# Two-layer image block on one core: the border between images rebuilt, and TensorE in written order

## The chip, the cores and the metric

The kernel runs on one core of a Trainium2 chip. A core has a matrix engine (TensorE, "PE" in the profile, with "PEld" for its weight loads), a vector engine (VectorE, DVE), an activation engine (ScalarE, ACT), a general engine (GpSimd, POOL) and an engine that here only issues transfers (SyncE, SP). Each engine takes its instructions in a fixed order, and waits for the others by semaphores. GpSimd, ScalarE and SyncE can each issue DMA transfers, on queues of their own. The metric is device time in microseconds, the median of several runs.

## What is computed

32 images of 96 channels x 56 x 56 pass through two layers. Both normalise each group of three channels, then add a branch to the image. Cut to what matters:

```python
# layer 0
v = gn(x)                                  # 32 groups of 3 channels
h = act_q(bn(conv1x1(v, quant(w1))))       # 96 -> 576 channels, 4 bits
h = act_q(bn(depthwise3x3(h, quant(w2))))  # 576 channels, 4 bits
x = x + v + bn(conv1x1(h, quant(w3)))      # 576 -> 96 channels
# layer 1, on v = gn(x), in three parts of 32 channels
x_0, x_05, x_1 = v[:32], v[32:64], v[64:]
x_0  = conv3x3(x_0, conv0_w * gate(mean(x_0)))                  # spatial
gap  = mean(x_05); alpha = 0.1 + 0.8 * sigmoid(mlp(gap))
Fre  = frft2d(x_05, F(alpha), F(alpha))                         # fractional Fourier
Mix  = conv1x1(Fre, conv05_w * gate(gap))
x_05 = abs(frft2d(Mix, F(-alpha), F(-alpha)))
x_1  = irfft2(conv1x1(rfft2(x_1), conv1_w * gate(mean(x_1))))   # Fourier
x = x + v + conv3x3(concat(x_0, x_05, x_1), conv2_w)            # 96 -> 96
```

## The kernel before

The outer loop takes the images one after the other. `layer0(i)` and `layer1(i)` don't issue anything; they return lists of steps (a cost and a function). `interleave` merges two lists by their costs, and so the convolution of image i is written out mixed with layer 1 of image i-1. The order of writing isn't the order on the engines: the framework's scheduler puts each engine's instructions in an order of its own, and pools of buffers add waits.

Layer 0 of an image, in the names of the profile:

- `norm`: bn_stats on VectorE, then `group_stats` (L284 on): two small matmuls (pma, pva) average over a group, and GpSimd takes the power -0.5 (L305). `split` and `base` make vh and vl, two parts of the normalised image in four phases (even and odd rows and columns).
- `expand(b, k)`: tile pe, 4 matmuls (L371), 20 of them (5 blocks b of 128 channels, 4 phases k). ACT quantises to qte (L312), DVE clips to q1s (L314), and four transfers (two in the last block) copy q1s into the padded tile qp, 32 channels each (L384; 72 copies per image, all issued by SP). There are two tiles qp.
- `depthwise(b, j)`: tile pd, 8 matmuls (L397), 18 of them, one for each 32 channels; it needs all four phases of its block in qp. ACT makes qtd, DVE makes q2.
- `project(h, lo, hi)`: tile pp (L413), two halves in four pieces each, then four DVE updates of x (L425), and `stats` (bn_stats, L429).

Layer 1 of an image: `norm` (pmb, pvb, then xs on DVE and ACT, L468 and L472; a copy flipped in both directions, called Jx here, on DVE, L479 and L487; the padded spatial part xq on ACT and DVE, L494 and L496), `gates` (ph, pg, pa, po, L500 to L519, with hid and the sigmoids on ACT, then products on DVE), `angles` (table by the sine on ACT, pj and pvv, L571 to L587, and vv sent into two rows of xs), `mix_t` (px, L608), `mix_f` (pm, L641, its result z goes to DRAM and comes back as zh and az), `spatial` (ps, L707), `hilbert` (pr), `rows_f` (pi, L667), `columns_f` (pz, L683), `final` (pc, L727, 7 chunks of 8 rows, each added to x by DVE at L735), and `store`.

Tiles pe, pd and pp share a pool of two PSUM buffers ("pair"); all small tiles, px to pc, share four ("bank"). ACT has to read a pe or pd before the next but one can start.

What is called the border here is the stretch from the last pp of one image to the last matmul of pvv of layer 1. Before, the border is written as `interleave(nxt["first"], one[-3:] + end)`: the first four expansions of the next image, the last three pc chunks of the previous one, and its store. The norm of layer 1 stands at the head of the next round, and the scheduler puts pc_4 to pc_6 ahead of pmb. The image is loaded and stored in three transfers each, issued by POOL, since the channel groups of 32 are kept in swapped order (`groups`, `perm`).

Of the kernel before, what the change touches and what calls it, by code (L numbers as in the profile page):

```python
# [59 lines left out]
HN = PN // 2  # L61
L = 57
# [38 lines left out]
def block_kernel(ctx: ExitStack, tc: tile.TileContext, out: bass.AP, a: dict):  # L101
# [21 lines left out]
    groups = ((0, 2 * G), (G, G), (2 * G, 0))  # L123
    xts = {}

    def load(i):
        xt = xp.tile([C, HW], F32, tag="x", name=f"x{i}")
        for p, c in groups:
            nc.gpsimd.dma_start(out=xt[p : p + G, :], in_=x_in[i, c : c + G].rearrange("c h w -> c (h w)"))
        xts[i] = xt  # L130
# [11 lines left out]
    def prepare():  # L142
# [90 lines left out]
        cw1 = signed("cw1", "coef1")  # L233
        cw2 = signed("cw2", "coef2")
        return w1, dw, w3, A1, B1, A2, B2, A3, B3, cw1, cw2

    w1, dw, w3, A1, B1, A2, B2, A3, B3, cw1, cw2 = prepare()
# [19 lines left out]
    for k in range(2):  # L257
        t = cp.tile([128, 4, PT], FP8, tag=f"qp{k}", name=f"qp{k}")
        nc.gpsimd.memset(t, 0.0)
        qps.append(t)  # L260
# [13 lines left out]
    g1s, css = [], []  # L274
# [3 lines left out]
    for k in range(2):  # L278
        t = cp.tile([128, 128], F32, tag=f"g1{k}", name=f"g1{k}")
        nc.scalar.dma_start(out=t[bias], in_=a["bias1"])  # L280
        nc.vector.tensor_tensor(t[bias], t[bias], bcoef[bias], ALU.mult)
        g1s.append(t)
        t = cp.tile([128, 3 * W], F32, tag=f"cs{k}", name=f"cs{k}")
        nc.vector.memset(t, 0.0)  # L284
        css.append(t)
# [38 lines left out]
    def layer0(i):  # L324
# [42 lines left out]
        def expand(b, k):  # L367
            ps = pair(f"pe{i}_{b}_{k}")
            for n, v in enumerate((s["vh"], s["vl"])):
                for h in range(2):  # L370
                    nc.tensor.matmul(  # L371
                        ps[:, h, :HN],
                        w1[:, 128 * b : 128 * (b + 1)],
                        v[:, k, HN * h : HN * (h + 1)],
                        start=(n == 0),
                        stop=(n == 1),
                    )
            src = q1s[turn["q1s"] % 3]
            turn["q1s"] += 1
            quant_act(ps, A1[:, b : b + 1], B1[:, b : b + 1], src[:, :, :PH], f"e{i}_{b}_{k}")  # L380

            n, at = blk(b) // G, PW * (k // 2) + k % 2
            for g in range(n):
                nc.sync.dma_start(  # L384
                    out=qps[(NB * i + b) % 2][G * k : G * (k + 1), g, at : at + PH * PW],
                    in_=src[g * G : (g + 1) * G].rearrange("c h w -> c (h w)"),
                )

        def depthwise(b, j):
            g = 4 * b + j  # L390
            if g == 0:
                s["q2"] = p1.tile([128, NG0, PN], BF16, tag="q2", name=f"q2_{i}")
            ps = pair(f"pd{i}_{g}")
            for t in range(4):
                for h in range(2):
                    at = PW * (t // 2 + PH // 2 * h) + t % 2
                    nc.tensor.matmul(  # L397
                        ps[:, h, :HN],
                        dw[:, g, t, :],
                        view(qps[(NB * i + b) % 2][:, j, :], at, [[PW, PH // 2], [1, PH]]),  # L400
                        start=(t == 0),
                        stop=(t == 3),
                    )
            quant_act(ps, A2[:, g : g + 1], B2[:, g : g + 1], s["q2"][:, g, :], f"d{i}_{g}")
# [26 lines left out]
        def first(b):  # L431
            return [(0.75, lambda k=k: expand(b, k)) for k in range(4)]

        conv = []
        for b in range(NB):
            part = []
            nxt = first(b + 1) if b + 1 < NB else []
            for k in range(max(len(nxt), blk(b) // G)):  # L440
                part += nxt[k : k + 1]
                if k < blk(b) // G:
                    part.append((1.45, lambda b=b, k=k: depthwise(b, k)))
            conv.append(part)
# [3 lines left out]
        last.append((0.0, stats))  # L448
# [3 lines left out]
            "first": first(0),  # L452
            "conv": conv,
            "last": last,
# [3 lines left out]
    def layer1(i):  # L458
# [3 lines left out]
        def norm():  # L462
# [4 lines left out]
            ff, fr = slice(0, G), slice(G, 2 * G)  # L467
# [6 lines left out]
            for at, src, dims in (  # L474
                (W + 1, n * W + n, [W, 1]),
                (1, n, [1]),
                (W, n * W, [W]),
            ):
                nc.vector.tensor_scalar(  # L479
                    view(xs[fr], at, [[d, n] for d in dims]),  # L480
                    view(xt[ff], src, [[-d, n] for d in dims]),
                    mean[ff],
                    rstd[ff],
                    ALU.subtract,
                    ALU.mult,
                )
            nc.vector.tensor_scalar(xs[fr, 0:1], xt[ff, 0:1], mean[ff], rstd[ff], ALU.subtract, ALU.mult)  # L487
            sp = slice(2 * G, C)
# [9 lines left out]
        def gates():  # L498
# [31 lines left out]
            for k in range(4):  # L530
                nc.vector.tensor_tensor(
                    view(tmp[fr], 128 * k, [[4, 32], [1, 4]]),
                    view(cw1[fr], 128 * k, [[4, 32], [1, 4]]),
                    view(sg[fr], 0, [[1, 32], [32, 4]]),
                    ALU.mult,
                )
            g1 = g1s[i % 2]
            nc.vector.tensor_reduce(g1[fr], view(tmp[fr], 0, [[4, 128], [1, 4]]), AX.X, ALU.add)

            for k in range(2):  # L540
                nc.vector.tensor_tensor(
                    view(tmp[: 2 * G], 128 * k, [[4, 32], [1, 4]]),
                    view(cw2, 128 * k, [[4, 32], [1, 4]]),
                    view(sg[: 2 * G], 128, [[1, 32], [32, 4]]),
                    ALU.mult,
                )
# [9 lines left out]
        def angles():  # L556
# [17 lines left out]
            cs = css[i % 2]  # L574
            s["cs"] = cs
# [39 lines left out]
        def hilbert(g):  # L615
# [10 lines left out]
            for r in range(4):  # L626
                src = ps[G * r : G * (r + 1), : 2 * W * n].rearrange("p (q u w) -> p q u w", u=2, w=W)
                at = (1 + 32 * g + 2 * r) * (W + 2) + 1
                dst = view(cat[:G].rearrange("p h w -> p (h w)"), at, [[8 * (W + 2), n], [W + 2, 2], [1, W]])
                if r % 2:  # L630
                    nc.vector.tensor_copy(dst, src)
                else:
                    nc.scalar.copy(dst, src)

        def mix_f(j):
# [5 lines left out]
            nc.tensor.matmul(ps[:, :CN], g1s[i % 2][2 * G : 3 * G + 2], s["xs"][2 * G : 3 * G + 2, at], start=True, stop=True)  # L641
# [19 lines left out]
        def rows_f(g):  # L661
# [4 lines left out]
            for k in range(4):  # L666
                nc.tensor.matmul(  # L667
                    ps[:W, 2 * W * k : 2 * W * (k + 1)], zh[:, 4 * g + k, :], s["cs"][: 64 + W, W : 3 * W], start=True, stop=True
# [5 lines left out]
        def columns_f(g):  # L674
# [5 lines left out]
            for k in range(n):  # L680
                q = 4 * (4 * g + k)
                for t in range(2):
# [3 lines left out]
                        s["cs"][:W, W * (1 - t) : W * (3 - t)],  # L686
# [16 lines left out]
        def spatial(h):  # L703
# [10 lines left out]
            for k in range(4):  # L714
                src = ps[G * k : G * (k + 1), :HN].rearrange("p (h w) -> p h w", w=PH)
                at = (1 + PH * h + k // 2) * (W + 2) + 1 + k % 2
                dst = view(cat[2 * G : C].rearrange("p h w -> p (h w)"), at, [[2 * (W + 2), PH // 2], [2, PH]])
# [19 lines left out]
        def store():  # L737
            for p, c in groups:
                nc.gpsimd.dma_start(out=out[i, c : c + G].rearrange("c h w -> c (h w)"), in_=xt[p : p + G, :])
# [12 lines left out]
    now = layer0(0)  # L752
    interleave(now["norm"] + now["split"] + now["first"], [])
    for i in range(B + 1):
        one, end = layer1(i - 1) if i else ([], [])
        if i == B:
            interleave(one + end, [])
            break
        if i + 1 < B:
            load(i + 1)  # L760
        conv, last, nxt = now["conv"], now["last"], None
        if i + 1 < B:
            nxt = layer0(i + 1)
            conv[1] += nxt["norm"]
            conv[4][1:1] = nxt["split"]
        interleave([s for part in conv for s in part] + last, one[:-3])
        interleave(nxt["first"] if nxt else [], one[-3:] + end)
        now = nxt
# [35 lines left out]
def _constants():  # L804
# [4 lines left out]
    perm = np.r_[64:96, 32:64, 0:32]  # L809
    k = {}  # L810
    group = perm // 3
# [29 lines left out]
    k["coef1"] = coef1.reshape(128, 512).astype(f)  # L841
# [8 lines left out]
    k["coef2"] = coef2.reshape(64, 256).astype(f)  # L850
    return perm, k


def _layout(inputs):
# [4 lines left out]
    perm, k = _constants()  # L859
# [11 lines left out]
    k["w1"][:, :HID] = g0("w1")[:, perm, 0, 0].T  # L871
# [12 lines left out]
    k["w3"] = np.tile(g0("w3")[perm, :, 0, 0].T.reshape(NG0, G, C).swapaxes(0, 1), (4, 1, 1)).reshape(128, NG0 * C)  # L884
# [3 lines left out]
    k["vec96"] = np.stack([g0(n)[perm] for n in ("b3", "g3", "be3", "m3", "v3")], axis=1)  # L888
# [5 lines left out]
    k["cw1"] = np.tile(by_parts(g1("conv05_w"))[None, :, None], (4, 1, 4, 1, 1)).reshape(128, 512)  # L894
# [4 lines left out]
    k["cw2"] = np.tile(by_parts(g1("conv1_w"))[None, :, None], (2, 1, 2, 1, 1)).reshape(64, 256)  # L899
# [3 lines left out]
    start = {"alpha": G, "gfreq": G, "gsp": 2 * G, "gfft": 0}  # L903
# [23 lines left out]
    k["wc"] = g1("conv2_w")[perm][:, perm].transpose(1, 2, 3, 0).reshape(C, 9 * C)  # L927
    k["bc"] = g1("conv2_b")[perm][:, None]
# [19 lines left out]
```

## Time and profile before

| what | value |
|---|---|
| median of 3 runs | 5584.15 us (5581.7 to 5593.18) |
| profiled execution | 5580.95 us |
| its span | 5579.2 us |
| mean granted clock of TensorE | 0.842 |
| one image, pmb to pmb (2023.2 to 2194.2 us) | 171.0 us |
| x loads: 96 of 392 KB, issue to landing | 6.0 us |
| out stores: 96 of 392 KB, issue to landing | 5.3 us |

A line of a group reads: line, engine, operation, output<-inputs, shape, count; then busy time and the mean of one in ns; then the engine's idle time just before these instructions and what ended most of it. "Clock" is the share of full speed that TensorE was granted: at 0.5 the same matmul takes twice as long, and counts as busy for all of it. An image is 1.2 MB, in three transfers of 392 KB each way.

### The profile page before, as it was taken

How to read it: one execution, taken by the hardware profiler on the slowest of the kernel's cores; microseconds unless marked ns; L12 is line 12 of the kernel's file. 1: busy time of each engine (PE TensorE's matmuls, PEld its weight loads, DVE VectorE, ACT ScalarE, POOL GpSimd, SP SyncE). 2: the span in 40 equal slices, each digit the busy share in tenths (PEclk: the TensorE clock that was granted, in tenths of full speed). 3: DMA queues.
4: the chain of work that ended last, by engine and by line, in shares of the span. 5: the costliest groups of instructions: out<-in, count | busy, mean ns of one | idle time of the engine just before them, and what ended most of it. 6: DMA issues, size and time to landing. Idle time of an engine off the chain costs nothing.

```text
span 5579.2 us, 65275 instructions
## 1 busy us (share of the span) xinstructions
PE 4954.7 (89%) x24384; PEld 3090.9 (55%) x24384; DVE 2410.1 (43%) x5355; ACT 2161.8 (39%) x2824; POOL 176.0 (3%) x270
## 2 busy tenths in 40 slices
PE   4988899889998898998889988889888899889897
PEld 2555555555555555555555555556555555555554
DVE  6444434444444444344444444444444434344432
ACT  3433434433334334344333443343443334433421
POOL 2000000000000000000000000000000000000000
PEclk9788888888988888888889888888888898888887
DMA  2121212221212212122212122121221121221111
GB/s 61 38 54 39 43 42 43 54 53 30 53 33 54 54 39 43 42 44 54 53 30 53 33 53 54 38 44 35 51 54 47 36 51 34 54 54 32 41 33 39
DMA packets 394080, 249.79 MB, mean 45 GB/s; under 512 B 284053, under 2 KB 386917, under 8 KB 387621
## 3 DMA queue, kind: packets, MB, share of 16 engines
q1 hardware_dynamic: 381696, 165.68, 13.8%
q0 software_dynamic: 9216, 77.08, 5.9%
q8 instruction: 194, 3.18, 0.2%
q10 hardware_dynamic: 2852, 2.85, 0.2%
q14 instruction: 122, 0.99, 0.1%
HBM read 92.77 MB, written 89.92 MB: 33 GB/s over the span
## 4 chain that ended last, share of the span: by engine, by line
PE 80%; ACT 9%; DMA 5%; DVE 4%; SPq 1%; issue 1%; ACTq 0%; POOL 0%; DVEq 0%; POOLq 0%
PE pc L727 27%; PE pd L397 16%; PE px L608 6%; PE pe L371 6%; PE ps L707 5%; PE pz L683 5%; PE pi L667 4%; PE pp L413 4%; ACT qtd L312 4%; DMA qp<-q1s 4%; PE pm L641 3%; SPq L384 1%; ACT xq L494 1%; ACT xs L472 1%; PE pr L625 1%
## 5 line engine op out<-in xcount | busy, mean ns | idle before, releaser
L727 PE MATMUL pc<-cat,wc 96*96 96x448 f32 x4032 | 1565.9, 540 | 1.0 <-ACT cat L701 1.0
L397 PE MATMUL pd<-qp,dw 128*128 128x392 fp8e4 x4608 | 1063.0, 378 | 393.3 <-DMA qp<-q1s 221.7
L727 PEld LDWEIGHTS pc<-cat,wc 96*96 96x96 f32 x4032 | 650.8, 163 | 766.4 <-issue 759.1
L312 ACT ACTIVATE qte<-pe,o,s 128x784 int16<-128x784 f32 x640 | 635.6, 998 | 1050.2 <-PE pe L371 618.6
L312 ACT ACTIVATE qtd<-pd,o,s 128x784 int16<-128x784 f32 x576 | 577.3, 1002 | 1024.3 <-PE pd L397 992.1
L397 PEld LDWEIGHTS <-dw 128*128 128x128 fp8e4 x4608 | 464.8, 105 | 892.1 <-issue 555.5
L371 PE MATMUL pe<-vh,w1r 96*128 96x392 f32 x1280 | 497.4, 474 | 26.1 <-ACT vh L360 21.7
L314 DVE TENSOR_SCALAR q<-qtd 128x784 bf16<-128x784 int16 x576 | 209.5, 364 | 711.1 <-ACT qtd L312 710.3
L735 DVE SCALAR_TENSOR_TENSOR x<-pc,bc,x 96x448 f32<-96x448 f32 x224 | 152.0, 679 | 784.6 <-PE pc L727 784.6
L314 DVE TENSOR_SCALAR q1s<-qte 128x784 fp8e4<-128x784 int16 x640 | 364.4, 570 | 276.9 <-ACT qte L312 255.0
L371 PE MATMUL pe<-vl,w1r 96*128 96x392 f32 x1280 | 366.2, 370 | 0.0
L608 PE MATMUL px<-g,xs 64*112 64x64 f32 x1792 | 351.4, 393 | 0.0
L608 PEld LDWEIGHTS px<-g,xs 64*112 64x112 f32 x1792 | 339.2, 302 | 19.3 <-issue 19.3
L371 PEld LDWEIGHTS pe<-vh,w1r 96*128 96x128 f32 x1280 | 273.0, 218 | 130.2 <-issue 71.3
L707 PE MATMUL ps<-xq,g 128*128 128x392 f32 x512 | 299.1, 749 | 0.0
L683 PE MATMUL pz<-cs,Y 56*128 56x112 f32 x1792 | 264.4, 318 | 13.7 <-ACT Y L671 13.7
L371 PEld LDWEIGHTS pe<-vl,w1r 96*128 96x128 f32 x1280 | 267.9, 214 | 0.4 <-DVE vl L361 0.4
L683 PEld LDWEIGHTS pz<-cs,Y 56*128 56x128 f32 x1792 | 255.9, 230 | 20.8 <-ACT Y L671 20.8
L641 PE MATMUL pm<-xs,g 34*128 34x448 f32 x448 | 222.9, 642 | 17.5 <-ACT zs L646 17.3
L667 PE MATMUL pi<-cs,zh 120*56 120x112 f32 x2048 | 211.9, 262 | 7.7 <-DMA zh<-z 7.7
L413 PE MATMUL pp<-q,w3q 32*96 32x392 bf16 x4608 | 212.3, 330 | 3.8 <-ACT qtd L312 2.8
L707 PEld LDWEIGHTS ps<-xq,g 128*128 128x128 f32 x512 | 145.2, 298 | 122.7 <-issue 112.0
(149 smaller groups left out, 4214.0 us busy)
## 6 DMA issues: line engine op xcount, KB each, us to landing
qp<-q1s SPq DMA_DIRECT2D x2304, 26.2 KB
z<-zs SPq DMA_DIRECT2D x224, 224.0 KB
x<-in_x_dram POOLq DMA_DIRECT2D x96, 392.0 KB, 6.0
out_dram<-x POOLq DMA_DIRECT2D x96, 392.0 KB, 5.3
zh<-z SPq DMA_DIRECT2D x64, 392.0 KB
az<-z SPq DMA_DIRECT2D x256, 98.0 KB
xs<-vv SPq DMA_DIRECT2D x64, 12.2 KB
prep<-in_w_dram ACTq DMA_DIRECT2D x1, 864.0 KB
```

The source lines that it names most:

```text
L312: nc.scalar.activation(t.rearrange("p (h n) -> p h n", h=2), ps[:, :, :HN], AF.Relu, bias=offset, scale=scale)
L314: nc.vector.tensor_scalar(dst, src, 15.0, None, ALU.min, saturate=False if dst.dtype == FP8 else None)
L371: nc.tensor.matmul(ps[:, h, :HN], w1[:, 128 * b : 128 * (b + 1)], v[:, k, HN * h : HN * (h + 1)], start=(n == 0), stop=(n == 1),)
L397: nc.tensor.matmul(ps[:, h, :HN], dw[:, g, t, :], view(qps[(NB * i + b) % 2][:, j, :], at, [[PW, PH // 2], [1, PH]]), start=(t == 0), stop ...
L413: nc.tensor.matmul(s["pp"][k // 2][:C, k % 2, :HN], w3[rows, g, :], s["q2"][rows, g, HN * h : HN * (h + 1)], start=(g == 0), stop=(g == NG ...
L608: nc.tensor.matmul(ps[: 2 * W, 64 * k : 64 * (k + 1)], s["xs"][: 2 * G, at : at + 2 * W], s["g2"], start=True, stop=True)
L641: nc.tensor.matmul(ps[:, :CN], g1s[i % 2][2 * G : 3 * G + 2], s["xs"][2 * G : 3 * G + 2, at], start=True, stop=True)
L667: nc.tensor.matmul(ps[:W, 2 * W * k : 2 * W * (k + 1)], zh[:, 4 * g + k, :], s["cs"][: 64 + W, W : 3 * W], start=True, stop=True)
L683: nc.tensor.matmul(ps[:, 2 * W * k : 2 * W * (k + 1)], s["Y"][:, t, q : q + 4, :].rearrange("p h c -> p (h c)"), s["cs"][:W, W * (1 - t) : ...
L707: nc.tensor.matmul(ps[:, :HN], s["g0"][:, 128 * k : 128 * (k + 1)], view(xq, PH // 2 * h * (W + 2) + k, [[W + 2, PH // 2], [2, PH]]), star ...
L727: nc.tensor.matmul(ps[:C, :CN], wc[:, C * t : C * (t + 1)], cat[:, CR * j + dy : CR * j + dy + CR, dx : dx + W], start=(t == 0), stop=(t = ...
L735: nc.vector.scalar_tensor_tensor(part, ps[:C, :CN], bc, part, ALU.add, ALU.add)
```

## The change

It does seven things:

1. The swapped order of channels goes (`groups`, `perm`), and with it the split in three: one load and one store per image, both issued by SP. The load of image i+2 is issued after the border, in place of image i+1's at the head of the round.
2. The flipped copy Jx is done by GpSimd.
3. Expansion runs seven steps ahead of the depthwise step (`LEAD = 7`): the first seven of 20 stand at the border, then one depthwise and one expansion in turn. There are three tiles qp.
4. The copies q1s to qp with odd number go by GpSimd's queue, those with even number by SP's (36 and 36 per image).
5. The tiles g1 and cs exist once and not twice; two coefficient tables are one.
6. The border is written with layer 1's norm first, then seven expansions with the last two pc chunks; the last pp pieces are mixed with pc_3 and pc_4. The next image's norm and split are at other places of the round.
7. `manual_schedule` for TensorE: its instructions are issued in the order written; the other engines are still ordered by the scheduler.

```diff
-        for p, c in groups:
-            nc.gpsimd.dma_start(out=xt[p : p + G, :], in_=x_in[i, c : c + G].rearrange("c h w -> c (h w)"))
+        nc.sync.dma_start(out=xt, in_=x_in[i].rearrange("c h w -> c (h w)"))
...
-    for k in range(2):
+    for k in range(3):
         t = cp.tile([128, 4, PT], FP8, tag=f"qp{k}", name=f"qp{k}")
...
-                nc.sync.dma_start(
-                    out=qps[(NB * i + b) % 2][G * k : G * (k + 1), g, at : at + PH * PW],
+                (nc.gpsimd if g % 2 else nc.sync).dma_start(
+                    out=qps[(NB * i + b) % 3][G * k : G * (k + 1), g, at : at + PH * PW],
                     in_=src[g * G : (g + 1) * G].rearrange("c h w -> c (h w)"),
...
+        ex = [(0.75, lambda b=b, k=k: expand(b, k)) for b in range(NB) for k in range(4)]
+        de = [(1.45, lambda g=g: depthwise(g // 4, g % 4)) for g in range(NG0)]
         conv = []
-        for b in range(NB):
...
+        for g in range(NG0):
+            conv += de[g : g + 1] + ex[LEAD + g : LEAD + g + 1]
...
-                nc.vector.tensor_scalar(
-                    view(xs[fr], at, [[d, n] for d in dims]),
+                nc.gpsimd.tensor_scalar(
+                    view(xs[G : 2 * G], at, [[d, n] for d in dims]),
...
     now = layer0(0)
+    if B > 1:
+        load(1)
     interleave(now["norm"] + now["split"] + now["first"], [])
...
-            conv[1] += nxt["norm"]
-            conv[4][1:1] = nxt["split"]
-        interleave([s for part in conv for s in part] + last, one[:-3])
-        interleave(nxt["first"] if nxt else [], one[-3:] + end)
-        now = nxt
+            conv[8:8] = nxt["norm"]
+            at = 2 * (4 * NB - LEAD) + 1
+            conv[at:at] = nxt["split"]
+        interleave(conv, one[:-4])
+        interleave(now["last"], one[-4:-2])
+        two, done = layer1(i)
+        interleave(two[:1] + (nxt["first"] if nxt else []), one[-2:] + end)
+        if i + 2 < B:
+            load(i + 2)
+        one, end, now = two[1:], done, nxt
+    interleave(one + end, [])
...
-    with tile.TileContext(nc) as tc:
+    with tile.TileContext(nc) as tc, tc.manual_schedule(engines={mybir.EngineType.PE}):
```

Written out, TensorE's work at the new border is: the last piece of pp, pmb, pvb, pc_5, the four pe of block 0, pc_6, three pe of block 1, pd_0, then ph, pg, pa, po, pj, pvv, then the fourth pe of block 1, px_0, pd_1, px_1 and so on.

## Prediction

> **What bounds the kernel now.** The page first: busy times, the chain that ended last, the costliest groups.
>
> ```profile
> PE   4954.7 (89%) x24384; PEld 3090.9 (55%) x24384; DVE 2410.1 (43%) x5355; ACT 2161.8 (39%) x2824; POOL 176.0 (3%) x270
> PE 80%; ACT 9%; DMA 5%; DVE 4%; SPq 1%; issue 1%; ACTq 0%; POOL 0%; DVEq 0%; POOLq 0%
> L397 PE MATMUL pd<-qp,dw 128*128 128x392 fp8e4 x4608 | 1063.0, 378 | 393.3 <-DMA qp<-q1s 221.7
> L312 ACT ACTIVATE qtd<-pd,o,s 128x784 int16<-128x784 f32 x576 | 577.3, 1002 | 1024.3 <-PE pd L397 992.1
> ```
>
> TensorE bounds it. It idles mostly before pd (393.3 us), of which the q1s copies end 221.7, or 7.2 per image. But busy is not busy at full speed, so the next view is one image cut into stages (pmb to pmb, 171.0 us; columns: stretch, length, PE, PEld, DVE, ACT, POOL busy, granted clock, DMA share, GB/s).
>
> ```profile
> 2023.20:2061.70 38.50, 25.34 (x98) 14.94 (x97) 20.69 (x52) 22.12 (x23) 3.54 (x7) 0.67 0.36 83
> 2061.70:2086.60 24.90, 24.18 (x97) 17.35 (x97) 9.34 (x20) 6.73 (x11) 0.00 (x0) 0.64 0.13 40
> 2086.60:2097.00 10.40, 10.40 (x50) 7.22 (x51) 3.81 (x8) 4.53 (x9) 0.00 (x0) 0.80 0.31 106
> 2097.00:2128.20 31.20, 28.69 (x182) 22.91 (x182) 11.82 (x34) 17.78 (x27) 0.56 (x1) 0.89 0.41 60
> 2128.20:2172.40 44.20, 44.20 (x273) 22.69 (x272) 22.52 (x44) 12.57 (x18) 0.00 (x0) 1.00 0.02 5
> 2172.40:2194.20 21.80, 21.74 (x68) 11.03 (x67) 6.02 (x12) 3.83 (x4) 0.56 (x2) 1.00 0.06 16
> ```
>
> TensorE works 154.55 of 171.0 us; 13.2 of the 16.45 idle lie in the first row, the border between images. By the matmul rows at full clock one image is: pc 7 x 6.77 = 47.4, pd 18 x 1.38 = 24.8, pe 20 x 0.713 = 14.3, pp 6.2, px 5.4, ps 5.4, pz 6.3, pi 6.4, pm 5.7, pr 3.3, small ones 2.5: 127.7. So 26.9 us are lost to half clock and 16.45 to waiting. Both prices matter.
>
> **What brings the clock back.** Cut into steps of 3.413 us on the grid of the clock's own changes, every step shows 1.0 or 0.5. It falls after a step with half or less to do. It doesn't rise after every full one. Two full steps that stayed at half (all engines), each followed by one that is still at half:
>
> ```profile
> 3657.53:3660.95 3.42, 3.42 (x11) 2.53 (x11) 2.35 (x6) 1.82 (x3) 0.00 (x0) 0.50 0.06 15
> 3660.95:3664.36 3.41, 3.41 (x6) 1.47 (x5) 0.00 (x0) 3.36 (x5) 0.00 (x0) 0.50 0.02 6
> ...
> 4268.52:4271.93 3.41, 3.27 (x11) 2.13 (x10) 3.38 (x6) 2.83 (x2) 0.00 (x0) 0.50 0.06 16
> 4271.93:4275.35 3.42, 2.34 (x10) 2.31 (x11) 2.30 (x10) 3.39 (x3) 0.00 (x0) 0.50 0.00 0
> ```
>
> The first held 1.85 us of ps (128 rows) and 1.64 of pz (56 rows): by rows 1.85 + 1.64 x 56/128 = 2.57 of 3.41. The second held 1.49 of pd and 1.77 of pe (96 rows): 2.82. Of 78 steps of px alone (64 rows) none raised it. Steps that did raise it begin at 2.85 (2.63 pd, 0.29 pe); ps alone did in 46 of 46. So the bar lies near 2.83, an estimate from these rows. No step of before starts at half clock with pc alone (96 rows): it would reach 3.41 x 0.75 = 2.56, under the bar, as would pe alone.
>
> **Part by part, per image.** The written order is: last pp, pmb, pvb, pc_5, four pe, pc_6, three pe, pd_0, gates ph to pvv, then px, pd and pe mixed, pm, ps.
>
> (a) Statistics. Before, pc_4 to pc_6 lie between the last pp and pmb. Now nothing does. Rows: four x updates 2.2, four bn_stats 2.2, bn_aggr 0.33, then pmb to pvb 1.15 and small steps: 6.1 us idle. Any grid of 3.41 us has a nearly empty step in it, so the clock is at half when pc_5 starts. Bounds 5.5 to 6.6.
>
> (b) pc_5 to pd_0 then hold 13.5 + 7 x 0.713 + 1.38 = 19.9 us of full-speed work, 96 rows but for the last 1.4. Below the bar all of it doubles: +19.9. If pc does raise the clock after one step, +3.4 (1.7 more work time, about as much lost again at the next boundary). I take 19.9, by the 2.57 row, the nearest to 2.56. One more us for pe_0_2, whose pair buffer waits for ACT.
>
> (c) Gates and angles. Before fills them in part; with TensorE in written order nothing stands between ph and pvv. The end of before shows this chain bare (columns: start, length, engine, operation, idle before):
>
> ```profile
> 5439.97 0.26 PE L500 MATMUL ph<-stb,mw 96*32 96x1 f32 x2 [1.75 <-DVE stb L306]
> 5440.57 1.22 PE L505 MATMUL pg<-mw,hid 33*1 33x320 f32 x2 [0.34 <-ACT hid L502]
> 5447.63 1.96 PE L518 MATMUL po<-row 1*128 1x64 f32 x8 [5.43 <-DVE row L510]
> 5454.44 0.76 PE L571 MATMUL pj<-de,e 57*128 57x112 f32 x2 [4.46 <-DVE de L569]
> 5456.87 0.96 PE L587 MATMUL pvv<-v 1*56 1x112 f32 x4 [1.21 <-DVE v L582]
> ```
>
> 17.9 us from ph to the end of pvv. Four of the 5.4 before po go away, since xs and xq are done under pc_5 now; 1.1 comes on, as hid waits behind qtd_0 on ACT: 15.0, of which 2.5 is work. Idle +12.5, bounds 10 (less DVE in it) and 15.4 (nothing saved).
>
> (d) px comes up cold. Between px's a pd lifts the clock if enough of its 2.8 us falls in one step (2.25, by the bar: in 1.67 of 3.41 positions). First chance pd_1, 6.7 us in, worth 3.3; then pd_2 (7.9), pd_3 (11.2). I take 6.
>
> (e) pm (34 rows) takes the clock down again until ps_0: from the second pe after it to ps_0 are about 8 us of work. I take 6.5, bounds 3 and 9.
>
> (f) Other waits of the fixed order, no filler behind them: pva 1, pi_0 for zh 1.5, pz_0 1, pc_0 1.1, pd_15 1, pp's buffers 2.4: 8, bounds 5 and 12.
>
> (g) What goes: with expansion seven steps ahead, copies are out for over 15 us before pd needs them, against 1.85 to 5.1 us each, so the 7.2 us on copies and 5.5 on qtd go; that idle isn't in the sum. Seven pe and pc_6 are the cover; without it 7.2 come back. pz with pd and pe keeps full clock, also in the sum.
>
> (h) At nothing: one load and one store from SP, the same 1.2 MB each way as three of 392 KB (landing 6.0 and 5.3 us). The load stands behind the store's landing on SP, and behind it qp copies and the vv rows; pm, the first reader of those, is over 20 us off. Half the copies go to POOL at 0.52 per issue against 0.58, behind Jx. Jx: 2.7 us on DVE; on POOL no such row. The nearest, pow against a small DVE step (0.57 to 0.15), makes it up to 10; DVE's own 2.7 is the other end. I take 6: its reader px_0 is 50 us later. If POOL holds DVE's xs back by that, ACT's xs and xq and then pe_0_0 are late, which pc_5 at half clock (13.5) covers; at full clock about 4 show.
>
> [...]
>
> Sum: 127.7 + 6.1 + 19.9 + 1 + 12.5 + 6 + 6.5 + 8 = 187.7 against 171.0. Around the 31 periods the span has 5579.2 - 31 x 171.0 = 278.2. 31 x 187.7 + 278 = 6097 of span; the profiled run took 1.75 more than its span and the median 3.2 more than it: **6102**. Ends of the terms together reach 5650 to 6600; as they are separate, 5900 to 6290 is the forecast's own range.
>
> [...]
>
> **Rivals.** (1) pc does bring the clock back, stalls as summed: 187.7 - 19.9 + 3.4 = 171.2, with 4 for Jx 175: 5590 to 5710. For: pc never fell below 1.0 where it was warm; against: the 2.57 row. (2) Faster: pc lifts the clock in its first step, and it then lasts through px and pm, as pd and pe between them do the rest: (d) 2, (e) 2, (f) 5: 171.2 - 4 - 4.5 - 3 = 159.7, 5234; it wins as long as (b), (d) and (e) together stay under 15.7 us, against 32.4 above. For: mixed steps at full clock stayed there down to 0.48 of full rows; against: image 0's mix of px, pd and pe stayed at half for 41 us. (3) The order isn't kept or hardly changes a thing: 171, within 0.2%; against: manual order is for all of TensorE.
>
> **Numbers.** Forecast 0.73, rival 1 0.10, rival 2 0.15, rival 3 0.02. No change means within 0.2% (11 us). Faster 0.16 (rival 2 and a little of 1), same 0.03, slower 0.81. The range takes in rival 1 from 5590 and stops at 6290.
>
> **What would show it.** After pvb, pc_5 at 13 us or more with clock 0.5; about 6 us idle before pmb and 12 inside ph to pvv, most of TensorE's idle on stb, row, de and v; idle on qp<-q1s near nothing; PE busy up to about 5300 us. Wrong if pc_5 takes 7 to 10 us, or if idle stays near 16 per image.

## The result, and the profile after

The changed kernel takes 6283.26 us (median of 4, 6252.87 to 6287.67) against 5585.95 in the runs beside it: a ratio of 1.1235, 95% interval 1.1197 to 1.1273. The profiled execution has a span of 6285.9 us and a mean clock of 0.806 (0.842 before). All ratios in this document are of fast runs alone, while the median of written_filled also holds two slow ones (5923 us without them).

First the page of the changed kernel, busy times and the chain that ended last, then three groups of instructions (line, engine, operation, tiles, count; busy us, mean ns; idle before and what ended it):

```profile
PE 5289.2 (84%) x24384; PEld 3099.5 (49%) x24384; DVE 2663.1 (42%) x5224; ACT 2180.1 (35%) x2824; POOL 1110.9 (18%) x1359
...
PE 73%; DVE 13%; ACT 8%; issue 4%; DMA 1%; POOL 0%; ACTq 0%; SPq 0%; POOLq 0%
...
L390 PE MATMUL pd<-qp,dw 128*128 128x392 fp8e4 x4608 | 1037.2, 378 | 9.5 <-ACT qtd L305 9.0
...
L364 PE MATMUL pe<-vh,w1r 96*128 96x392 f32 x1280 | 503.9, 481 | 345.0 <-ACT qte L305 322.9
...
L452 DVE TENSOR_SCALAR xs<-x,stb 32x3136 f32<-32x3136 f32 x32 | 387.0, 12094 | 1.1
```

Two things went up: TensorE's idle time (span less busy: 996.7 us against 624.5), and its busy time (5289.2 against 4954.7) for the same 24384 matmuls, which is mostly time at half clock: busy time weighted by the granted clock grew only from 4219 to 4346 us. VectorE is now 13% of the chain (4%). The old wait is gone, pd idles 9.5 us instead of 393.3. A new one stands before pe, 322.9 us on ACT's qte. The last line tells where to look: VectorE's xs, one instruction per image, takes 12.1 us on average, and took 1.9 in the kernel before:

```profile
L468 DVE TENSOR_SCALAR xs<-x,stb 32x3136 f32<-32x3136 f32 x32 | 60.9, 1903 | 1.1
```

The waits of TensorE in the changed kernel (us in all, times, longest):

```profile
PE pe L364 <- ACT qte L305: 322.9, 63, 16.7
PE pmb L287 <- DVE mvb L285: 157.5, 32, 4.9
PE pj L554 <- DVE de L552: 156.5, 32, 4.9
...
PE pd L390 <- DMA qp<-q1s: 0.4, 1, 0.4
```

The second and third are the statistics chain and the gates chain, standing bare once in each of 32 images. One image cut into stages, from the last pp to the next last pp (length; PE, PEld, DVE, ACT, POOL busy; clock, DMA share, GB/s):

```profile
2061.06:2067.50 6.44, 0.83 (x6) 0.74 (x5) 5.29 (x12) 0.00 (x0) 0.00 (x0) 0.72 0.00 0
2067.50:2104.13 36.63, 26.91 (x74) 14.38 (x74) 19.76 (x15) 13.14 (x10) 20.90 (x16) 0.72 0.13 35
2104.13:2116.59 12.46, 4.73 (x26) 2.93 (x25) 8.57 (x30) 4.58 (x7) 1.81 (x4) 0.67 0.60 152
2116.59:2163.03 46.44, 45.66 (x131) 26.81 (x131) 11.71 (x31) 11.54 (x16) 4.49 (x9) 0.50 0.15 48
2163.03:2201.07 38.04, 36.61 (x244) 27.17 (x242) 15.52 (x34) 24.16 (x36) 5.48 (x11) 1.00 0.35 55
2201.07:2258.53 57.46, 54.71 (x290) 26.12 (x290) 21.54 (x41) 14.55 (x20) 1.49 (x3) 0.94 0.02 4
```

The rows are: statistics; pc_5 to pd_0; gates and angles; px to ps_0; pr to ps_1; pc_0 to the last pp. The border (rows 1 to 3) holds 23.1 us of idle, and row 4 runs whole at half clock: 45.66 us busy for some 22.8 of work. From row 5 on little is lost. After the first, the images take from 191 to 198 us; this one, of 197.5, is among the longer ones.

Inside row 2, the timeline of the changed kernel (start, length, engine, operation):

```profile
2067.50 10.30 PE L708 MATMUL pc<-cat,wc 96*96 96x448 f32 x18
...
2068.66 14.62 POOL L463 TENSOR_SCALAR xs<-x,stb 32x3025 f32<-32x3025 f32 x3
2068.77 12.10 DVE L452 TENSOR_SCALAR xs<-x,stb 32x3136 f32<-32x3136 f32 x1
...
2080.88 0.16 DVE L455 SCALAR_TENSOR_TENSOR nmr<-stb 96x1 f32<-96x1 f32 x1
2080.96 2.18 DVE L480 TENSOR_SCALAR xq<-x,stb 32x1512 f32<-32x1512 f32 x2
2081.14 2.99 ACT L456 ACTIVATE xs<-x,nmr,stb 32x3136 f32<-32x3136 f32 x1 [42.95 <-DVE nmr L455]
...
2084.14 3.35 ACT L478 ACTIVATE xq<-x,nmr,stb 32x1568 f32<-32x1568 f32 x2
2087.52 1.90 ACT L305 ACTIVATE qte<-pe,o,s 128x784 int16<-128x784 f32 x2
...
2088.58 0.70 PE L364 MATMUL pe<-vh,w1r 96*128 96x392 f32 x1 [9.34 <-ACT qte L305]
```

VectorE's xs starts 0.1 us after GpSimd's Jx and ends 12.1 us later. Behind it stands nmr, for which ACT waits; then ACT does its own xs and xq (6.3 us) and only then qte. pe_0_2 waits 9.34 us for that with both its buffers full. And pc_5 itself takes 10.3 us, neither the 6.8 of full clock nor the 13.5 that was expected of it.

### The profile page after: what moved, and what is told of

Its sections match the earlier page's. It is cut to its first block, busy times and chain, and to the rows that moved or that the text cites. A ratio compares the mean times of both kernels' runs of the same rounds, so it can differ in the third digit from the quotient of the medians.

```text
span 6285.9 us, 66280 instructions
## 1 busy us (share of the span) xinstructions
PE 5289.2 (84%) x24384; PEld 3099.5 (49%) x24384; DVE 2663.1 (42%) x5224; ACT 2180.1 (35%) x2824; POOL 1110.9 (18%) x1359
## 4 chain that ended last, share of the span: by engine, by line
PE 73%; DVE 13%; ACT 8%; issue 4%; DMA 1%; POOL 0%; ACTq 0%; SPq 0%; POOLq 0%
PE pc L708 22%; PE pd L390 15%; PE pe L364 8%; PE px L589 6%; PE pm L622 6%; DVE xs L452 4%; PE pz L664 4%; PE pp L406 4%; PE pi L648 3%; DVE x L418 2%; PE ps L688 2%; ACT qtd L305 2%; ACT xq L478 2%; ACT cat L682 2%; ACT qte L305 2%
## 5 line engine op out<-in xcount | busy, mean ns | idle before, releaser
L708 PE MATMUL pc<-cat,wc 96*96 96x448 f32 x4032 | 1721.9, 585 | 32.6 <-ACT cat L682 32.6
L377 POOL DMA_DIRECT2D qp<-q1s x1152 | 586.0, 512 | 3382.9 <-DVE q1s L307 2202.3
L708 PEld LDWEIGHTS pc<-cat,wc 96*96 96x96 f32 x4032 | 706.0, 178 | 945.9 <-issue 894.6
L390 PE MATMUL pd<-qp,dw 128*128 128x392 fp8e4 x4608 | 1037.2, 378 | 9.5 <-ACT qtd L305 9.0
L364 PE MATMUL pe<-vh,w1r 96*128 96x392 f32 x1280 | 503.9, 481 | 345.0 <-ACT qte L305 322.9
L456 ACT ACTIVATE xs<-x,nmr,stb 32x3136 f32<-32x3136 f32 x32 | 95.8, 2994 | 1368.1 <-DVE nmr L455 1368.1
L463 POOL TENSOR_SCALAR xs<-x,stb 32x55 f32<-32x55 f32 (+1 forms) x96 | 467.7, 5119 | 3.6
L364 PE MATMUL pe<-vl,w1r 96*128 96x392 f32 x1280 | 399.0, 399 | 0.0
L452 DVE TENSOR_SCALAR xs<-x,stb 32x3136 f32<-32x3136 f32 x32 | 387.0, 12094 | 1.1
L622 PE MATMUL pm<-xs,g 34*128 34x448 f32 x448 | 363.5, 956 | 0.0
L406 PE MATMUL pp<-q,w3q 32*96 32x392 bf16 x4608 | 246.6, 335 | 87.7 <-DVE x L418 62.2
## 6 DMA issues: line engine op xcount, KB each, us to landing
qp<-q1s SPq DMA_DIRECT2D x1152, 26.2 KB
qp<-q1s POOLq DMA_DIRECT2D x1152, 26.2 KB, 1.8
```

Source lines behind the costliest of these rows:

```text
L364: nc.tensor.matmul(ps[:, h, :HN], w1[:, 128 * b : 128 * (b + 1)], v[:, k, HN * h : HN * (h + 1)], start=(n == 0), stop=(n == 1),)
L377: (nc.gpsimd if g % 2 else nc.sync).dma_start(out=qps[(NB * i + b) % 3][G * k : G * (k + 1), g, at : at + PH * PW], in_=src[g * G : (g + 1 ...
L390: nc.tensor.matmul(ps[:, h, :HN], dw[:, g, t, :], view(qps[(NB * i + b) % 3][:, j, :], at, [[PW, PH // 2], [1, PH]]), start=(t == 0), stop ...
L406: nc.tensor.matmul(s["pp"][k // 2][:C, k % 2, :HN], w3[rows, g, :], s["q2"][rows, g, HN * h : HN * (h + 1)], start=(g == 0), stop=(g == NG ...
L452: nc.vector.tensor_scalar(xs[2 * G : 3 * G], xt[fr], mean[fr], rstd[fr], ALU.subtract, ALU.mult)
L463: nc.gpsimd.tensor_scalar(view(xs[G : 2 * G], at, [[d, n] for d in dims]), view(xt[ff], src, [[-d, n] for d in dims]), mean[ff], rstd[ff], ...
```

## The experiments

All are timed against the kernel before on the same chip. Idle is the span of the profiled run less TensorE's busy time.

| run | median us | ratio to before, 95% | idle us | clock |
|---|---|---|---|---|
| before | 5584 | | 624.5 | 0.842 |
| the change | 6283 | 1.124 (1.120 to 1.127) | 996.7 | 0.806 |
| jx_on_vector | 5791 | 1.037 (1.035 to 1.039) | 705.5 | 0.849 |
| pc5_before_norm | 6240 | 1.120 (1.115 to 1.124) | 1129.2 | 0.816 |
| scheduler_order | 5516 | 0.988 (0.987 to 0.990) | 436.7 | 0.857 |
| gates_spread | 6076 | 1.090 (1.086 to 1.094) | 939.0 | 0.831 |
| written_filled | 5982 | 1.060 (1.056 to 1.065) | 754.2 | 0.833 |
| written_jx_gates | 5810 | 1.040 (1.038 to 1.042) | 670.8 | 0.847 |
| sched_jx_vector | 5294 | 0.950 (0.946 to 0.953) | 335.3 | 0.882 |
| sched_jx_vector_sp | 5357 | 0.958 (0.955 to 0.961) | 290.6 | 0.866 |
| sched_jx_vector_lead4 | 5297 | 0.949 (0.947 to 0.950) | 315.8 | 0.873 |
| sched_lead4_two_qp | 5302 | 0.948 (0.946 to 0.951) | 314.7 | 0.872 |
| sched_jx_vector_lead10 | 5784 | 1.035 (1.034 to 1.037) | 737.1 | 0.869 |
| before_jx_gpsimd | 5789 | 1.036 (1.035 to 1.038) | 759.5 | 0.825 |

### Jx alone

```diff
-                nc.gpsimd.tensor_scalar(
+                nc.vector.tensor_scalar(
                     view(xs[G : 2 * G], at, [[d, n] for d in dims]),
```

> The changed kernel with one edit: the flipped copy Jx is back on VectorE. In the changed kernel's trace VectorE's xs took 12.1 us beside Jx on GpSimd (14.6 us), against 1.9 us before, and TensorE then idled 9.3 us ahead of pe_0_2. Theory 1 (the two engines hold each other up): xs takes about 1.9 us again, Jx 2.7 on VectorE, the 9.3 us wait shrinks to under 2, and the clock doesn't fall there, which gives pe_0_2, pe_0_3 and pc_6 back some 3 us: 11 to 12 us an image, 5910 to 5945. Rival (ACT's own xs and xq, 6.4 us, hold pe_0_2 up): a wait of 6 or more stays and the time is 6180 to 6290.

Measured 5791, 492 us under the change, 15.9 an image and more than the 11 to 12 of theory 1. xs takes 1.90 us again; the wait of pe for qte falls from 322.9 to 34.7 us. The rival falls. Of the profiled run's gain, 9.1 us an image are idle time and 6.6 busy time: the clock was down for longer behind the wait than the 3 us that theory 1 allowed. Its timeline shows why nothing is left: ACT is through with xq at 2093.56, and pe_0_0 starts at 2093.59. The groups of VectorE and the waits, of this run:

```profile
L452 DVE TENSOR_SCALAR xs<-x,stb 32x3136 f32<-32x3136 f32 x32 | 60.9, 1903 | 1.1
```

```profile
PE pmb L287 <- DVE mvb L285: 157.5, 32, 4.9
PE pj L554 <- DVE de L552: 156.5, 32, 4.9
...
PE pe L364 <- ACT qte L305: 34.7, 63, 6.5
```

The same edit put into the kernel before, the other way round:

```diff
-                nc.vector.tensor_scalar(
+                nc.gpsimd.tensor_scalar(
                     view(xs[fr], at, [[d, n] for d in dims]),
```

> The kernel before with one edit: Jx on GpSimd. Theory 1 (GpSimd and VectorE hold each other up; before's TensorE waits at the border for ACT and copies behind it): VectorE's xs or xq takes 10 us longer, and 0 to 6 us of that an image reach TensorE: 5584 to 5770. Rival (the hold-up comes from the order of the changed kernel, not from Jx): VectorE's busy time and the time as before or up to 1% less, since VectorE loses 2.7 us of work.

Measured 5789, 203 us over the kernel before, 6.5 an image: just past the upper end of theory 1, and the rival falls. The scheduler puts other work beside Jx here, so that xs, at 2.5 us on average, is hardly held, and other instructions are. At TensorE the cost shows as pd's wait for the copies, 312.2 us against 221.7, and pe's for qte, 28.5 against 2.9. The timeline of this run shows the hold-up in its plainest form:

```profile
2096.30 10.56 POOL L479 TENSOR_SCALAR xs<-x,stb 32x3025 f32<-32x3025 f32 x1
...
2102.95 4.14 DVE L314 TENSOR_SCALAR q<-qtd 128x784 bf16<-128x784 int16 x1 [7.18 <-ACT qtd L312]
...
2106.84 1.31 POOL L129 DMA_DIRECT2D x<-in_x_dram  x2
2107.01 0.55 DVE L314 TENSOR_SCALAR q1s<-qte 128x784 fp8e4<-128x784 int16 x1
```

An instruction of 0.36 us (the mean of this group before) begins at 2102.95, and ends at 2107.09, just after GpSimd's instruction (2106.86). The loads of x also stand behind Jx on GpSimd here; no wait of TensorE is put down to them, but no run set them apart from the hold-up.

### Who orders TensorE

```diff
-    with tile.TileContext(nc) as tc, tc.manual_schedule(engines={mybir.EngineType.PE}):
+    with tile.TileContext(nc) as tc:
```

> The changed kernel with one edit: the scheduler and not the written order decides TensorE's order. Theory 1 (the written order is the main loss, since the statistics and gates chains stand bare in it): idle around pmb and between ph and pvv falls to about what it was before; Jx on GpSimd still costs up to 10 us an image: 5600 to 5900. Rival (the loss comes from Jx, the longer lead or the copies, whatever the order): over 6100.

Measured 5516, under the expected span and 1.2% under the kernel before, with Jx still on GpSimd. The written order costs 767 us, more than the 697 by which the change is slower; without it the change is a gain. (With Jx on VectorE in both, the next run gives 5791 against 5294: there the written order costs 497.) The scheduler writes pe_0_0 to pe_1_0 ahead of pmb, and pc_5 and pc_6 behind pvb; pmb's wait on mvb falls to one of 4.9 us, pj's on de to 30.1. The hold-up hasn't gone, it has moved to xq, as this run's timeline shows:

```profile
2164.85 1.90 DVE L452 TENSOR_SCALAR xs<-x,stb 32x3136 f32<-32x3136 f32 x1
2165.23 14.78 POOL L463 TENSOR_SCALAR xs<-x,stb 32x3025 f32<-32x3025 f32 x3
2166.77 0.16 DVE L455 SCALAR_TENSOR_TENSOR nmr<-stb 96x1 f32<-96x1 f32 x1
2166.84 12.30 DVE L480 TENSOR_SCALAR xq<-x,stb 32x1512 f32<-32x1512 f32 x2
2167.02 2.99 ACT L456 ACTIVATE xs<-x,nmr,stb 32x3136 f32<-32x3136 f32 x1 [3.10 <-DVE nmr L455]
```

Here xs had begun before Jx and took its 1.90 us; nmr ran beside Jx in 0.16; xq was held: the first of its two instructions took 11.20 us instead of 1.08. GpSimd took longer too: xs, begun first, ran on for 1.52 us beside Jx, and the large part of Jx took 11.98 us instead of 10.56. So ACT starts 2.2 us after xs and not 12.4, which is why the same hold-up costs less in this order. With both edits:

> The changed kernel with the scheduler's order and Jx on VectorE. In the scheduler's order with Jx on GpSimd the hold-up is there too, on xq (12.3 us for two instead of 2.2), but TensorE has 13.5 us of pc after pvb to cover it. Theory 1 (cover hides the hold-up): within 1% of 5516, 5460 to 5570. Rival (the hold-up costs an image 10 us whatever lies beside it): 5180 to 5250.

Measured 5294: the hold-up costs 222 us in this order too, 7.2 an image. Theory 1, that pc hides it, falls, and so does the rival's full 10 us. This version beats both kernels, by 5.0% (4.7 to 5.4) and 16%. Its page and its waits on pd:

```profile
PE 4945.0 (94%) x24384; PEld 3006.4 (57%) x24384; DVE 2382.5 (45%) x5352; ACT 2174.6 (41%) x2825; POOL 717.3 (14%) x1231
```

```profile
PE pd L390 <- ACT qtd L305: 127.4, 221, 4.9
...
PE pd L390 <- ACT qte L305: 9.5, 31, 0.9
```

No wait for copies is left among them, and TensorE idles 335.3 us.

### Filling the written order by hand

```diff
+        interleave([], one[-2:-1])
-        interleave(two[:1] + (nxt["first"] if nxt else []), one[-2:] + end)
+        interleave(two[:1] + (nxt["first"] if nxt else []), one[-1:] + end)
```

> The changed kernel with one edit: pc_5 is written ahead of layer 1's norm, so that the statistics chain (6.4 us of idle TensorE) lies behind it. Theory 1 (idle and what the clock loses by it are both the cost): the 6.4 us go and pc_5 takes 6.8 instead of 10.3; but the wait ahead of pe_0_2, which comes from xs and Jx, is uncovered by as much as pc_5 had hidden and grows to about 12 us. From the last pp to the end of pd_0 38 us instead of 43: 6283 - 31 x 5 = about 6120. Rival (statistics cost their idle and nothing is uncovered): 31 x 10 less, 5970.

Measured 6240, a gain of 44 us where 160 was expected. The wait on mvb goes from 157.5 to 4.8 us, but pe's on qte rises from 322.9 to 399.9, as theory 1 had it (12.66 us for pe_0_2 in one image), and pd, which waited for next to nothing, now waits 187.1 us in the two lines below, of which the second names no releaser:

```profile
PE pe L364 <- ACT qte L305: 399.9, 33, 16.7
...
PE pd L390 <- DMA qp<-q1s: 136.8, 22, 7.1
...
PE pd L390 <- issue: 50.3, 8, 6.6
```

pc_6 had stood between the first four expansions and pd_0; moved ahead, it no longer covers the copies. There is more to it in this trace: with pc_6 done earlier the store goes out earlier, and so does the load behind it on SP, now ahead of block 0's last copies. The copies that GpSimd issued within 1.2 us behind a load (58 of them) took 8.05 us to landing by the median, those with no load or store in the 9 us before 1.75; and in 29 images pd_0 stood 5.8 to 7.1 us and began 8.4 to 9.7 us after the load was issued. In the image shown of the changed kernel the load follows pd_0, by 5.5 us. No run moved the load alone, so what it costs by itself is not shown. Next, the gates in six steps:

```diff
-        steps = [(0.5, norm), (2.0, gates), (1.0, angles)] + each(2.1, mix_t, 4) + each(0.8, mix_f, NCH)
+        small = (gate_hid, gate_rows, gate_outer, angles, angle_sums, angle_outer)
+        steps = [(0.5, norm)] + [(2.0, f) for f in small] + each(2.1, mix_t, 4) + each(0.8, mix_f, NCH)
```

> The changed kernel with one edit: gates and angles are cut into six steps, with one pd or pe written between two of them, still in written order. Theory 1 (the bare chain from ph to pvv, 12.5 us, costs its idle and takes the clock down for px, pd, pe and pm behind it, 46 us at half clock): idle falls by 4 to 8 us and part of the half-clock time goes: 5800 to 6050. Rival (px and pm take the clock down by themselves, so that only idle is won): 6030 to 6160, with the same 40 to 46 us at half clock behind pvv.

Measured 6076, 207 us won: a time in the rival's range, but not by the rival's way, since the half-clock time from pvv to the end of ps_0 fell from 42 to 29 us an image. Theory 1 was right in that part and wrong in the other: idle fell by 1.8 us an image only. The wait on de falls from 156.5 to 37.8, the clock rises from 0.806 to 0.831. But the steps that now stand between the gates are missing later: pc_0's wait for cat rises from 32.6 to 98.2 us. All three edits together, and two of them:

> The changed kernel, still in written order, with three edits together: Jx on VectorE, pc_5 ahead of layer 1's norm, gates and angles spread over pd and pe. Theory 1 (written order loses by what it leaves bare, Jx by the hold-up, and the two add): 5791 with Jx on VectorE alone, less 6.4 us of idle and 3.5 of clock at pmb and less the 6.7 us that spreading the gates brought, 16.6 an image: 5276, anything from 5250 to 5450. Rival (what is won at one place is lost at the next wait, as pc_5 ahead of the norm alone brought 44 us in all): 5600 to 5750.

> Written order, Jx on VectorE, gates spread over pd and pe; pc_5 and pc_6 where the change put them (the run with all three edits took 5982, against 5791 with Jx on VectorE alone). Theory 1 (moving pc_5 did the harm: pc_6 no longer stands between the first four pe and pd_0, and pd_0 waits 7.4 us for the copies with the clock down): 5791 less the 6.7 us an image of the spread gates, about 5584, 5530 to 5650. Rival (the spread gates did it, since pc_0 now waits 3.2 us for cat and the clock falls there): over 5800.

Neither came out as theory 1 had it, and the first took longer than its rival said, too (5982, or 5923, against 5600 to 5750). The gains don't add: with Jx on VectorE, spreading the gates brings nothing (1.040 against 1.037), and pc_5 ahead of the norm costs another 2% (1.060). In the trace of the three together, pd_0 of the image shown stands 7.4 us with the clock at half, and SP has issued the load of x just ahead of block 0's last copies:

```profile
1963.64 0.53 SPq L127 DMA_DIRECT2D x<-in_x_dram  x1
...
1964.22 10.44 SPq L377 DMA_DIRECT2D qp<-q1s  x8
1964.38 0.85 PE L364 MATMUL pe<-vl,w1r 96*128 96x392 f32 x2
...
1971.87 1.15 DVE L325 BATCH_NORM_STATS2 bn<-x 96x6 f32<-96x448 f32 x2 [6.38 <-DMA x<-in_x_dram]
...
1972.61 2.77 PE L390 MATMUL pd<-qp,dw 128*128 128x392 fp8e4 x8 [7.37 <-issue]
```

The two copies of GpSimd next behind the load, issued at 1964.13 and 1964.71, land at 1972.12 and 1972.48, and pd_0 begins at 1972.61. Those issued at 1961.64 and 1962.12, ahead of it, took 2.1 and 2.0 us. So theory 1 of written_jx_gates named the right wait, and without it, at 5810, the loss is smaller; yet the spread gates bring nothing there: pc_0 waits 94.9 us in all for cat (31.3 with Jx on VectorE alone), and from pc_0 to the next pmb 7.9 us an image run at half clock (2.1), as the rival said.

### What the rest of the change brings

sched_jx_vector holds every other edit of the change and is 5.0% faster than before. Three runs take those edits back one by one:

```diff
-                (nc.gpsimd if g % 2 else nc.sync).dma_start(
+                nc.sync.dma_start(
```

> As the scheduler's order with Jx on VectorE, with one more edit: all 72 copies of an image are issued by SP as before. Theory 1 (the lead of seven, not the second queue, takes the wait for the copies away): within 0.7% of the run with two queues. Rival (SP's issue, 0.58 us each, 42 us an image in bursts of four, is what pd waited for): 2% or more slower, and the wait for qp<-q1s rises from some 60 us back towards 220.

Measured 5357, 1.2% slower by the medians (0.958 against 0.950). It lies between the two: pd waits 4.9 us for copies in all, so the queue isn't what pd waited for, yet the second queue is worth something. The loss, in the profiled runs, is in busy time (5037.8 against 4945.0, clock 0.866 against 0.882); how it comes to that wasn't followed up.

```diff
-LEAD = 7
+LEAD = 4
```

> Scheduler's order, Jx on VectorE, the lead cut from seven expansions to four, as before; three qp and two queues stay. Theory 1 (the lead is what took the wait for copies away): pd waits for qp<-q1s again, 100 to 200 us in all, and the time is 5380 to 5500 against 5294. Rival (the third qp and the second queue do it): within 1% of 5294.

Measured 5297, as with seven. The rival holds this far: the lead isn't it. Then the third tile qp as well:

```diff
-    for k in range(3):
+    for k in range(2):
         t = cp.tile([128, 4, PT], FP8, tag=f"qp{k}", name=f"qp{k}")
```

> Scheduler's order, Jx on VectorE, a lead of four and two tiles qp, as before; what stays of the change is the one load and store, the second queue for copies, and the place of norms and border in the writing. Theory 1 (the third qp is what lets pd run without waiting): pd waits for qp<-q1s again by 100 us or more and the time is 5370 to 5500 against 5297. Rival (the load and store out of the copies' way and the second queue did it, not the buffer): within 1% of 5297.

Measured 5302, no difference again; pd waits 14.4 us for copies. So neither lead nor buffer gave the gain under the scheduler. What is left of the 5%, beyond the second queue, are the single load and store on SP, the new places of the steps in the writing and the single tiles and tables; these weren't told apart.

> Scheduler's order, Jx on VectorE, a lead of ten. Theory 1 (with more expansions at the border the gates chain has more to cover it): 5220 to 5290. Rival (seven is enough, and longer runs of expansions wait for ACT, 1.0 us each against 0.7): 5290 to 5400.

Measured 5784, and no verdict on the lead: with ten, block 3's expansions are written ahead of pd_3, which still reads block 0 from the same one of three tiles qp, so pd reads other data there, and the ordering that this forces isn't that of a longer lead.

## Why the prediction was right in its range, and where its steps were not

The forecast was 6102, its range reached to 6290, and 6283 came: slower, 181 us more than the sum and 7 below the range's end. By image that is 193.8 us ((6285.9 - 278) / 31) against 187.7. The image cut above, at 197.5, is 9.8 over the sum; term by term, in it:

- (a), statistics: 6.1 us forecast from the last pp to pc_5, 6.44 measured, 5.61 of it idle, clock down within (0.5 from 2063.96 on, behind a step with 0.52 of its 3.41 us busy; in before each of the 127 falls of the clock came behind a step with at most 0.55 of full rows). Right, and taken away it goes (pmb's wait 157.5 to 4.8).
- (b), pc below the bar: wrong. "Below the bar all of it doubles: +19.9" fails. The clock came back inside pc_5 in the image shown, at the end of the second step of it. Three steps of that image, then pc's own share of the first two (all engines, then pc alone):

```profile
2067.37:2070.79 3.42, 3.42 (x7) 1.57 (x8) 2.33 (x3) 0.00 (x0) 2.69 (x2) 0.50 0.00 0
2070.79:2074.20 3.41, 3.41 (x5) 1.20 (x5) 3.41 (x1) 0.00 (x0) 3.41 (x1) 0.50 0.00 0
2074.20:2077.61 3.41, 3.41 (x11) 1.49 (x9) 3.41 (x1) 0.00 (x0) 3.41 (x1) 1.00 0.00 0
```

```profile
2067.37:2070.79 3.42, 3.29 (x5) 1.50 (x6) 0.50 0.00 0
2070.79:2074.20 3.41, 3.41 (x5) 1.20 (x5) 0.50 0.00 0
```

  A step with 3.29 us of pc didn't raise the clock, the next, full of pc, did. Over the execution 56 of 64 steps at half clock that were full of pc raised it. The estimate of 2.83 full rows in 3.41 rested on giving pe and px the weight of their rows; pc at 2.56 passes, so rows alone aren't the measure. pc_5 lost 3.5 us and pc_6 1.8, not 6.8 each. The prediction's own sign of being wrong, pc_5 at 7 to 10 us, was missed by little here (10.30) and seen elsewhere: of 29 images 8 had 8.9 us, the others 10.0 to 10.4.
- (h), Jx: "at nothing", about 4 us with pc_5 at full clock: wrong, and the largest single error. The hold-up, 10.2 us of VectorE, reached TensorE as a wait of 9.34 us ahead of pe_0_2, and the clock fell a second time (0.5 from 2081.02 on, behind a step with 1.63 us busy). The hold-up was larger than the 6 us taken, and pc_5, with the clock back, a shorter cover: with pc_5 at the forecast 13.5 and two pe at half clock the wait would have been some 4.7 us, an estimate from these rows. Undone it gives 15.9 us an image back. It filled most of what (b) had put too high: from pvb to the end of pd_0 the sum had 40.8 us (2 x 19.9 + 1), the trace has 36.6. That the total was near is luck: errors of opposite sign.
- (c), gates: 12.46 us against 15.0, idle 7.7: oversized by 2.5. The chain was priced by its bare run at the end of before, all at half clock; here its first matmuls ran at full clock (pg 0.70 and po 1.21 us against 1.22 and 1.96), which is 1.7 of the 2.5, and the idle was a little shorter than the sum had it.
- (d) and (e), px and pm cold: 6 + 6.5 forecast, 22.8 measured: mis-sized by 10, the largest term behind the 9.8. "2.25, by the bar: in 1.67 of 3.41 positions" fails twice. Of 154 half-clock steps of the trace with px and pd none raised the clock, and only 6 of them held 2.0 us or more of pd. Two of these held 2.34 and 2.37 us of pd, over the 2.25, and stayed at half (in before all five with px and 2.41 or more rose). And the positions aren't free: in the 28 images from the third to the thirtieth, each of the three pd between and behind px begins 1.8 to 3.0 us into a step, where the end of the step cuts it. Why the alignment repeats is not shown.
- (f), other waits: 8 forecast, about 5 found (0.8, 1.4 and 2.8 in rows 4 to 6), the lower end. In row 6 a wait of pp also took the clock down for two steps, 3.3 us that no term held.
- The base of 127.7 us of work at full clock was too low, and had no bounds. Less the 19.9 and 2.5 of rows 2 and 3 it leaves 105.3 for rows 4 to 6; their busy time, half-clock time counted half, is 22.8 + 36.6 + 51.4 = 110.8. Over the whole execution busy time weighted by the clock is 131.8 us an image before and 135.8 after: part was missed in the rows of before (pd at 26.2, not 24.8), part came with the new order (pe 14.4 to 16.0, pp 6.4 to 7.3, pz 6.4 to 7.2).
- (g): right. pd's wait for copies fell from 221.7 to 0.4 us, and the stretch with pi and pz ran at 1.00. But pc5_before_norm shows that pc_6 was part of that cover, as (g) said, and under the scheduler the wait goes without the lead. The single load, at nothing in (h), cost nothing visible in the changed kernel (pd's 0.4 us of waiting for copies in all); where it went out ahead of block 0's last copies, in pc5_before_norm, those behind it took 8.05 us to landing by the median against 1.75, and pd waited 136.8 us in all for copies.

Rival 1 had pc's effect on the clock right and Jx too cheap; rival 2's condition, (b), (d) and (e) under 15.7 us together, was not met, (d) and (e) alone took 22.8. The first step of the prediction, that the bare chains of a written order cost more than the copies' waits it removes, is what scheduler_order confirms: 767 us, and 497 with Jx on VectorE.

## What to carry to other kernels

Jx moved to GpSimd wasn't off the path here: VectorE's xs beside it took 12.10 us instead of 1.90, and Jx back on VectorE was worth 15.9 us an image in the written order and 7.2 in the scheduler's. Before such a move look for the next VectorE instruction on the chain, and count what is left of GpSimd's against it in the estimate. An order written by hand must name a filler for each chain of small steps, and each filler taken from elsewhere is a cover removed there, and can bring a large transfer forward ahead of small ones (pc5_before_norm: 8.05 us to landing behind the load, 1.75 with none near); compare with the scheduler's order before keeping it. Two wrong terms of opposite sign can sum to a good forecast, so check terms by stage, not the total.

## What the runs showed of the hardware that was not expected

- These VectorE instructions, started while GpSimd worked on Jx, ended 1.65, 0.83 and 0.23 us after its large part and took 12.10 (xs in the change), 11.20 (xq in scheduler_order) and 4.14 us (q in before_jx_gpsimd) against 1.90, 1.08 and 0.36. Not every one was held: nmr ran beside it in 0.16 (scheduler_order). What makes the difference is not shown. Jx took 14.6 us on GpSimd in the changed kernel (2.6 on VectorE), 10.56 of it for its large part; its two small parts took 2.4 us on average there and 0.78 in before_jx_gpsimd.
- In the changed kernel steps at half clock full of pc (96 rows, f32) didn't always bring the clock back: 56 of 64 did; of 23 with 3.0 to 3.4 us of pc, 11 did. Of 154 at half clock with px and pd none did.
- Copies of 26 KB issued just behind the load of a whole image took 8.05 us to landing by the median, against 1.75 (pc5_before_norm).
